# Four head pairs instead of two taken by query halves at the end of a decoder layer, and the order that goes with it

## Chip, core and metric

The kernel runs on one NeuronCore of a Trainium2 chip. The metric is the time of one execution on the device in microseconds (us). TensorE is called PE, VectorE DVE, ScalarE ACT, GpSimd POOL and SyncE SP, as in the profile.

## What is computed

One post-norm decoder layer for 8 batches of 512 rows of width 256: causal linear attention in chunks of 32, cross-attention with 16 heads of 64, and a feed-forward layer with ternary weights and a low-rank gate, each followed by a layer norm of x plus the result.

```python
# linear attention
S = einsum('bncd,bnkd->bnck', Qc, Kc) * mask
out = sigmoid(x @ W_g.T) * O @ W_o.T + x
# cross-attention, 16 heads of 64
a = softmax(einsum('bmhd,bnhd->bhmn', qw, kw) / sqrt(64), axis=-1)
o = einsum('bhmn,bnhd->bmhd', a, vw).reshape(B, M, 1024);  return o @ Wo + bo
# feed-forward: ternary w_fc and w_proj, low-rank gate
h = bitlinear(x, w_fc) + gate * (x @ v.T @ fast_b.T @ u.T)
r = maximum(h, 0);  return bitlinear(r * r, w_proj)
```

## The kernel before

Values of full precision are carried as two fp16 parts (high and low), and products take three passes (high-high, high-low, low-high). Eight batches follow each other. For each batch the steps are:

- `gen_l0`: the linear attention, up to the first norm and the transposed rows `x1T`.
- `gen_kv`, `gen_q`, `gen_v`: keys, queries and values of a head pair (tiles `W`, `v`).
- `scores(u)` for a unit u = (batch, head pair, quarter of the queries; 128 queries): six PE matmuls into two PSUM banks `s`; on DVE per head one custom instruction that adds the mask and takes the minimum (`s`, `nm`), called a score reduction below; on ACT per head one exponential (`e`, with its sum in `den`).
- `split_p`: `e` into the fp16 parts `ph` (high part on ACT or POOL, low part on DVE) and a DMA transpose `pT<-ph` on SP, for two quarters at a time.
- `attend(u)`: 24 small PE matmuls per unit into `av`. With all four quarters in place: division by `den` on DVE (`of`), high part on ACT (`oh`), low part on POOL, a DMA transpose on SP into `oT`.
- `gen_wo`: output projection (`pwo`), second norm, `x2T`; `gen_ffn`: the feed-forward layer (`pz`, `zst`, `ph`, `r`, `rh`, `py`), then the third norm in `ffn_end`.

Work of the neighbouring batches is pulled between the units as filler: projections and the linear attention of batch b+1, output projection and feed-forward of batch b-1.

The last batch (7) ends differently. Its pairs 6 and 7 are "tail" pairs: the units run pair 6 quarters 0 and 1, pair 7 quarters 0 and 1, then the same for quarters 2 and 3. For a tail pair `attend` finishes each half of the queries by itself, with 256-wide instructions and a transpose by PE (`ofl`, `ohl`, `pTo`, copies into `oT` by ACT and DVE). `gen_wo_part` adds the output projection of pairs 0 to 3 early (`pwp`), `wo_tail(i)` that of pairs 4 to 7 for half i (`pwl`) with the second norm (`b`) and its transposes (`pTb`, `x2T`), and `ffn_tail(b, i)` the feed-forward layer of half i, called f0 and f1 below (`pz`, `ph`, `r4` as `r`, `rhl`, `pyl`, `yl`, third norm `c`, output).

The order on each engine is fixed when the program is built. All operations are first recorded (line 454 is the one place that then issues them, so nearly every row of the profile says L454) with a priority: the number of the unit plus offsets. A list scheduler then plays time forward with fixed costs per operation and takes on each engine the ready operation of the lowest priority. `OFF` holds offsets by engine and tile, `TP` those of the tail, `REACH` says how far in priority an engine may look past an operation whose port is taken, `PULL` how much filler is taken per unit. Any change of these numbers can permute the order all over the program.

The end of the recording, before the change:

```python
rest(len(pend) - 4)
wo_tail(0)
f0, f1 = ffn_tail(b, 0, U + TP[1], TP[2]), ffn_tail(b, 1, U + TP[3], TP[4])
go(f0, 3)
...
wo_tail(1)
go(f0, 1)
go(f1, 2)
```

Of the kernel before, what the change touches and what calls it, by code (L numbers as in the profile page):

```python
# [38 lines left out]
OFF = {"ACT th": -0.28, "ACT zst": -1.63, "ACT r": 0.81, "PE pTp": 1.99, "SP pT": 1.41, "ACT sph": 0.41, "DVE zf": 0.49, "PE ph": 0.16, "POOL ph": -1.37, "PE pwp": -0.46, "PE pTb": 2.45, "PE pb": 3.1, "POOL xh": 2.55, "ACT rh": 1.56, "PE pu": 0.39, "ACT row": 1.53, "PE po": -0.14, "PE pwl": 1.81, "SP xs": 0.62, "PE pss": -0.66, "DVE wqkv": -0.5, "DVE fct": -3.44, "ACT oh": -1.55, "DVE sp": 1.14, "POOL rhl": 0.12, "POOL oh": -0.82, "PE pyl": -0.58, "PE pz": -2.5, "PE pp": 0.13, "DVE mvb": -0.45}  # L39
# [436 lines left out]
def decoder_kernel(ctx: ExitStack, tc: tile.TileContext, ins: dict, out: bass.AP):  # L476
# [191 lines left out]
    def setup_ffn():  # L668
# [19 lines left out]
        for i in range(2):  # L688
# [22 lines left out]
        nc.gpsimd.memset(vst, 0.0)  # L711
        split(vst[:, :, 0:RANK], vst[:, :, 96:96 + RANK], sv, WS)
        for g in (32, 64):
            nc.scalar.copy(vst[:, :, g:g + RANK], vst[:, :, 0:RANK])

# [6 lines left out]
        fbs = cst.tile([RANK, 2, 128], F16, name="fbs")  # L722
        nc.gpsimd.memset(fbs, 0.0)
        split(fbs[:, 0, 0:RANK], fbs[:, 1, 0:RANK], fb, 1.0)
        for g in (32, 64, 96):
            nc.scalar.copy(fbs[:, :, g:g + RANK], fbs[:, :, 0:RANK])
        uT = t4("uT", [RANK, 2, HID], F16)
# [7 lines left out]
        for n in range(2):  # L735
# [81 lines left out]
    def to_T(b, row, nm, xT, t0=0, nt=4, fast=False):  # L817
        if fast:
            xf = xT.rearrange("p a c (t n) -> p (a c) t n", t=4)
            for t in range(t0, t0 + nt):  # L820
                xs = wk.tile([128, 2, D], F16, tag="W", name=f"xs{nm}{b}{t}", bufs=4) if b else t4(f"xs{nm}{b}{t}", [128, 2, D])
                nc.scalar.copy(xs[:, 0], row[:, t])
# [167 lines left out]
    def ffn_h(b, j, ts, zst, nm, tail=False):  # L990
# [5 lines left out]
        nc.tensor.matmul(ps, ust[:, js], zst, start=False, stop=True)  # L996
        r4 = wk.tile([128, 256], F32, tag="E", name=f"r4{nm}{j}", bufs=3) if tail else tmp2(f"r4{nm}{j}", [128, ts.stop - ts.start])
        nc.scalar.activation(r4, ps, AF.Relu, scale=sfc4[:, j:j + 1])
# [37 lines left out]
    def ffn_tail(b, i, base, step_):  # L1036
        row = rows[b]
        rh, py = {}, {}
        ts = slice(256 * i, 256 * i + 256)

        rhl = wk.tile([128, 8, 2, 256], F16, tag=("pT", "ph")[i], name=f"rhl{i}", bufs=(PTS, PHS)[i])
        PL = 3
        for s_ in range(8 + PL):
# [3 lines left out]
            if s_ < 8:  # L1047
                j = s_
                r4 = ffn_h(b, j, ts, zst, f"{b}_{i}", True)
                hl = rhl[:, j]  # L1050
                if i == 0 or j % 2:
# [20 lines left out]
        for t in range(2):  # L1072
            tt = 2 * i + t
            y = tmp2(f"yl{tt}", [128, D])
            nc.vector.tensor_tensor(y, py[t], s2b, ALU.mult)
# [13 lines left out]
    def scores(u):  # L1089
# [10 lines left out]
        if qt == 0:  # L1100
            den[b, p] = wk.tile([128, 4, 2], F32, tag="den", name=f"den{b}_{p}", bufs=3)
        e = wk.tile([128, 2, T], F32, tag="E", name=f"e{b}_{p}_{qt}", bufs=3)
# [38 lines left out]
    def attend(u):  # L1141
        b, p, qt = u
        tail = b == B - 1 and p >= NP - 2
        if qt == 0 or (qt == 2 and tail):
# [122 lines left out]
    def step(u):  # L1267
        nonlocal last
        e = scores(u) if u is not None else None
        if last is not None:  # L1270
            nc.prio = now[0] + LATE["s"]
            split_p(*last)
            pend.append(last[0])
        last = (u, e) if u is not None else None

    for i, u in enumerate(units):
# [29 lines left out]
        if qt == 3:  # L1306
# [18 lines left out]
    def wo_tail(i):
        ps = misc(f"pwl{i}")
        for t in (2 * i, 2 * i + 1):
            o = (t - 2 * i) * D
            for p in range(NWP, NP):
                mm(ps[:, o:o + D], lambda k, a: oT[b, p][:, a, t * 128:(t + 1) * 128], lambda k, c: wo[:, p, c, :], 1,  # L1330
                   first=(p == NWP), last=(p == NP - 1))
            nc.vector.scalar_tensor_tensor(row[:, t, :], ps[:, o:o + D], 1.0 / (WS * WS), row[:, t, :], ALU.mult, ALU.add)
            layernorm(b, row, EPS, "b", t, 1, True)
            to_T(b, row, "b", x2T[b], t, 1, True)

    def go(g, n):
        for _ in range(n):
            next(g, None)

    def rest(n):  # L1340
        for _ in range(n):
            if pend:
                attend(pend.pop(0))

    at(U, TP[6])
# [4 lines left out]
    f0, f1 = ffn_tail(b, 0, U + TP[1], TP[2]), ffn_tail(b, 1, U + TP[3], TP[4])  # L1350
    go(f0, 3)
    at(U, 0)
    rest(2)
    go(f0, 3)
    at(U, 0)
    rest(2)
    go(f0, 2)
    at(U, 0)
# [53 lines left out]
```

## Time and profile before

| | |
|---|---|
| time, median of 3 runs | 1062.17 us (1061.53 to 1063.61) |
| the profiled execution's own time | 1060.95 us |
| its span | 1058.8 us (2.15 us lie around it) |
| mean granted PE clock | 0.994 |
| PE matmul busy | 994.6 us (94%), 11976 instructions |
| DVE busy | 985.8 us (93%), 2087 instructions |
| ACT busy | 884.5 us (84%), 1885 instructions |
| POOL busy | 568.7 us (54%), 518 instructions |

How to read it: busy times of one engine are unions of its instructions' spans. A DVE or ACT instruction's span overlaps the next one's by some 0.08 to 0.1 us, so the step from one start to the next is shorter than the duration shown. PE spans are pipelined as well: twelve matmuls of 512 columns by 64 rows show 1.47 us, and one shows 0.38 us. "Idle before" in brackets names the instruction that ended a wait. The span has four parts: set-up up to the first scores (DVE works on them at 49.5 us), eight batches of which the inner ones take some 123.5 us each, and, from 1011.8 us on, when the last score reduction is over, the tail of 47.0 us.

### The profile page before, as it was taken

To read this page: it belongs to the slowest core of one execution; us is meant where nothing else is said; L and a number is where in the kernel's file an instruction comes from. 1 tells how busy PE (TensorE), PEld (TensorE's weight loads), DVE (VectorE), ACT (ScalarE), POOL (GpSimd) and SP (SyncE) were. 2 spreads that over 40 slices of the span, in tenths; PEclk is the share of its full clock that TensorE was granted. 3 is DMA by queue.
4 is the path that set the end of the run, shared out by engine and by line. 5 is a ranking of instruction groups with operands and counts; after the bars stand their busy time and mean duration, and the time that the engine had idled before them with its cause. 6 is when DMAs were issued, how large, how long until landed. Compare 5 with 4: busy or idle time off the path is not lost.

```text
span 1058.8 us, 29904 instructions
## 1 busy us (share of the span) xinstructions
PE 994.6 (94%) x11976; PEld 636.0 (60%) x11976; DVE 985.8 (93%) x2087; ACT 884.5 (84%) x1885; POOL 568.7 (54%) x518
## 2 busy tenths in 40 slices
PE   6987879999999999999999999999999999999996
PEld 4544545665666566765567656665567655565574
DVE  6998999999899989999899999999899998999886
ACT  6797978899986998789987899869987899878846
POOL 0255284256842587344952579425873449424646
PEclk9999999999999999999999999999999999999999
DMA  8359999999999999989999899999999899999971
GB/s 289 119 107 195 186 191 197 178 155 185 194 172 201 164 177 180 203 155 187 173 193 201 158 167 196 187 196 153 180 182 209 147 187 160 187 203 164 174 124 41
DMA packets 646635, 185.64 MB, mean 175 GB/s; under 512 B 628448, under 2 KB 641376, under 8 KB 646496
## 3 DMA queue, kind: packets, MB, share of 16 engines
q1 hardware_dynamic: 644144, 183.34, 94.5%
q8 instruction: 93, 1.52, 0.6%
q10 hardware_dynamic: 2352, 0.40, 0.2%
q14 instruction: 46, 0.38, 0.1%
HBM read 21.18 MB, written 4.19 MB: 24 GB/s over the span
## 4 chain that ended last, share of the span: by engine, by line
PE 48%; DVE 24%; POOL 8%; DMA 8%; ACT 5%; issue 5%; SPq 1%; ACTq 0%; POOLq 0%; DVEq 0%
PE s L454 9%; PE av L454 9%; DVE s L454 8%; DVE ph L454 6%; PE pwo L454 6%; PE pvv L454 5%; PE pk L454 4%; PE pq L454 4%; DMA pT<-ph 4%; PE py L454 3%; DVE W L454 2%; POOL xsa L454 2%; ACT e L454 2%; POOL row L454 2%; PE pxa L454 2%
## 5 line engine op out<-in xcount | busy, mean ns | idle before, releaser
L454 ACT ACTIVATE e<-s,nm 128x512 f32<-128x512 f32 x512 | 350.5, 696 | 79.8 <-DVE nm L454 72.2
L454 DVE SCALAR_TENSOR_TENSOR ph<-e,ph 128x1024 f16<-128x1024 f32 x256 | 334.6, 1310 | 22.7 <-ACT ph L454 20.5
L454 DVE CUSTOM_DVE_ANT_0 s<-s,mb 128x512 f32<-128x512 f32 x512 | 342.1, 706 | 11.0 <-PE s L454 10.0
L454 PEld LDWEIGHTS <-pT 128*128 128x128 f16 x6144 | 197.5, 98 | 60.6 <-issue 37.6
L454 PE MATMUL av<-v,pT 128*128 128x64 f16 x6144 | 212.3, 194 | 12.0 <-DMA pT<-ph 9.7
L454 PE MATMUL s<-W 64*128 64x512 f16 x1536 | 207.4, 379 | 10.7 <-ACT e L454 8.8
L454 ACT ACTIVATE ph<-e 128x1024 f16<-128x1024 f32 x186 | 198.2, 1071 | 2.0
L454 POOL TENSOR_SCALAR ph<-e 128x1024 f16<-128x1024 f32 x70 | 87.5, 1250 | 203.9 <-ACT e L454 187.7
L454 POOL TENSOR_TENSOR oh<-of,oh 128x512 f16<-128x512 f32 x62 | 99.3, 1602 | 92.3 <-ACT oh L454 86.6
L454 PEld LDWEIGHTS <-W 64*128 64x128 f16 x1536 | 64.6, 94 | 108.6 <-issue 53.9
L454 PEld LDWEIGHTS <-wqkv 128*128 128x128 f16 x768 | 68.6, 98 | 88.3 <-issue 27.2
L454 PE MATMUL pk<-ctxh,wqkv 128*128 128x512 f16 x384 | 97.9, 383 | 11.9 <-POOL ctxh L454 8.8
L454 ACT ACTIVATION_READ_ACCUMULATOR e<-s,nm 128x1 f32 x512 | 108.3, 211 | 0.0
L454 PE MATMUL pvv<-wqkv,ctxh 128*128 128x256 f16 x768 | 97.9, 274 | 0.2 <-ACT e L454 0.2
L454 PE MATMUL pq<-x1T,wqkv 128*128 128x512 f16 x384 | 96.1, 380 | 1.3 <-DVE x1T L454 0.7
L454 POOL TENSOR_TENSOR rh<-r,rh 128x512 f16<-128x512 f32 x56 | 76.1, 1367 | 21.2 <-ACT rh L454 20.7
L454 PEld LDWEIGHTS <-oT 128*128 128x128 f16 x768 | 73.4, 98 | 20.9 <-issue 4.8
L454 PEld LDWEIGHTS <-ctxh 128*128 128x128 f16 x768 | 72.8, 98 | 17.4 <-issue 5.9
L454 PE MATMUL pwo<-wo,oT 128*128 128x256 f16 x672 | 82.0, 273 | 0.8 <-ACT e L454 0.5
L454 DVE DVE_READ_ACCUMULATOR2_ANT nm<- 128x1 f32 x512 | 70.0, 137 | 0.0
L454 PE MATMUL ph<-x2T,tfc 128*128 128x512 f16 (+1 forms) x288 | 67.3, 355 | 0.3 <-DVE of L454 0.2
L454 PE MATMUL py<-tpj,rh 128*128 128x256 f16 x448 | 60.3, 273 | 1.3 <-ACT rh L454 1.2
(190 smaller groups left out, 1485.6 us busy)
## 6 DMA issues: line engine op xcount, KB each, us to landing
row<-in_x SPq DMA_DIRECT2D x8, 512.0 KB, 5.8
xs<-in_xT SPq DMA_DIRECT2D x7, 512.0 KB, 4.5
ctxs<-in_ctxT SPq DMA_DIRECT2D x7, 512.0 KB, 4.1
out_dram<-row SPq DMA_DIRECT2D x7, 512.0 KB, 3.5
wqs<-in_wqkv SPq DMA_DIRECT2D x6, 512.0 KB, 8.1
pT<-ph SPq DMA_TRANSPOSE x131, 7.6
wos<-in_wo SPq DMA_DIRECT2D x4, 256.0 KB, 3.2
fcs<-in_w_fc SPq DMA_DIRECT2D x2, 512.0 KB, 4.5
```

Source lines behind the costliest of these rows:

```text
L454: getattr(real[x.engine], x.method)(*[r(a) for a in x.args], **{k: r(a) for k, a in x.kw.items()})
```

## The change

- `NT = 4`: pairs 4 to 7 of batch 7 are tail pairs (before: 6 and 7). The units run quarters 0 and 1 of pairs 4, 5, 6, 7, then quarters 2 and 3 of them. Pairs 4 and 5 take the 256-wide path and PE transposes too.
- `wo_tail(0)` and the generator of f0 are recorded as soon as the first halves of all tail pairs are attended (`start_half`), f0 with a priority from that unit on, and two steps of f0 are taken per unit after that. `wo_tail(1)` and f1 are recorded after f0 is complete; before, f0, `wo_tail(1)` and f1 were recorded interleaved.
- Buffers: f0's `r4` and all `rhl`, `yl`, `ofl`, `ohl`, `xs` tiles use other pools; `den` has 5 buffers instead of 3.
- Set-up: three `memset`, `pjn` (two instructions) from POOL to DVE; the copies `identh`, `s2b`, two `vst`, three `fbs`, two `ust` from ACT to DVE.
- Scheduler numbers: `REACH` 11.86 to 10.35, `PULL["g"]` 4.5 to 4.45, the filler `bw` 3.0 to 8.0 and from pair 7 on, new `TP`, and `OFF` entries for `pTb`, `pu`, `pwl`, `oh` (ACT), `pp` changed and for `x` (SP), `mvc`, `rstdc` added.

```diff
-REACH = 11.86
+REACH = 10.35
...
-TP = (-1.12, 2.0, 1.04, 3.04, 0.1, 5.1, 2.67)
+NT = 4
+FP = 2.0
+TP = (0.0, 1.0, 0.1, 2.0, 0.4, 5.0)
...
-PULL = {"k": 4.41, "l": 2.62, "w": 3.61, "f": 4.71, "g": 4.5}
+PULL = {"k": 4.41, "l": 2.62, "w": 3.61, "f": 4.71, "g": 4.45}
...
-        nc.gpsimd.memset(mdec, 0.0)
+        nc.vector.memset(mdec, 0.0)
...
-        nc.scalar.copy(identh, ident)
+        nc.vector.tensor_copy(identh, ident)
...
-            nc.gpsimd.tensor_scalar(neg, st, th[:, 1:2], None, ALU.is_lt)
+            nc.vector.tensor_scalar(neg, st, th[:, 1:2], None, ALU.is_lt)
...
-        nc.scalar.copy(s2b, pb[:, :D])
+        nc.vector.tensor_copy(s2b, pb[:, :D])
...
-            nc.scalar.copy(ust[64:96, sl], tl[64:96])
+            nc.vector.tensor_copy(ust[64:96, sl], tl[64:96])
...
-        tail = b == B - 1 and p >= NP - 2
+        tail = b == B - 1 and p >= NP - NT
...
+                if p == NP - 1:
+                    pT["done"] = True
...
-    units[-8:] = [(B - 1, p, qt) for q2 in (0, 2) for p in (NP - 2, NP - 1) for qt in (q2, q2 + 1)]
+    units[-4 * NT:] = [(B - 1, p, qt) for q2 in (0, 2) for p in range(NP - NT, NP) for qt in (q2, q2 + 1)]
...
+    def start_half(i):
+        bw.drain()
+        at(i, 1)
+        bf.drain()
+        at(i, TP[0])
+        wo_tail(0)
+        half["f0"] = ffn_tail(B - 1, 0, i + TP[1], TP[2])
...
             for _ in range(BURST - pend[0][2] % BURST):
                 attend(pend.pop(0))
+                if u[0] == B - 1 and "f0" not in half and (B - 1, NP - 1) in av and (B - 1, NP - 1, 1) not in pT and pT.get("done"):
+                    start_half(i)
         at(i, 0.0)
+        if "f0" in half:
+            go(half["f0"], 2)
+            at(i, 0.0)
...
-        if b == B - 1 and p == 6 and qt == 0:
+        if b == B - 1 and p == 7 and qt == 0:
             bw.add(0.0, gen_wo_part, b, NWP)
-        bw.pull(3.0)
+        bw.pull(8.0)
...
+    f0, f1 = half["f0"], ffn_tail(B - 1, 1, U + TP[3], TP[4])
+    at(U, 0)
+    while pend:
+        attend(pend.pop(0))
     at(U, TP[0])
-    rest(len(pend) - 4)
-    wo_tail(0)
...
+    go(f0, 20)
+    at(U, TP[0])
     wo_tail(1)
-    go(f0, 1)
     go(f1, 2)
-    go(f0, 1)
     at(U, TP[5])
-    ffn_end(b - 1)
-    go(f0, 9)
+    ffn_end(B - 2)
     go(f1, 20)
```

More of the change, by code (lines that the diff above doesn't have):

```diff
@@ L35 @@
 NWP = 4
-TP = (-1.12, 2.0, 1.04, 3.04, 0.1, 5.1, 2.67)
+NT = 4
+FP = 2.0
+TP = (0.0, 1.0, 0.1, 2.0, 0.4, 5.0)
 STICK = 2.09
 HOLD = 0.18
-OFF = {"ACT th": -0.28, "ACT zst": -1.63, "ACT r": 0.81, "PE pTp": 1.99, "SP pT": 1.41, "ACT sph": 0.41, "DVE zf": 0.49, "PE ph": 0.16, "POOL ph": -1.37, "PE pwp": -0.46, "PE pTb": 2.45, "PE pb": 3.1, "POOL xh": 2.55, "ACT rh": 1.56, "PE pu": 0.39, "ACT row": 1.53, "PE po": -0.14, "PE pwl": 1.81, "SP xs": 0.62, "PE pss": -0.66, "DVE wqkv": -0.5, "DVE fct": -3.44, "ACT oh": -1.55, "DVE sp": 1.14, "POOL rhl": 0.12, "POOL oh": -0.82, "PE pyl": -0.58, "PE pz": -2.5, "PE pp": 0.13, "DVE mvb": -0.45}
+OFF = {"ACT th": -0.28, "ACT zst": -1.63, "ACT r": 0.81, "PE pTp": 1.99, "SP pT": 1.41, "ACT sph": 0.41, "DVE zf": 0.49, "PE ph": 0.16, "POOL ph": -1.37, "PE pwp": -0.46, "PE pTb": 1.59, "PE pb": 3.1, "POOL xh": 2.55, "ACT rh": 1.56, "PE pu": 1.49, "ACT row": 1.53, "PE po": -0.14, "PE pwl": 2.75, "SP xs": 0.62, "PE pss": -0.66, "DVE wqkv": -0.5, "DVE fct": -3.44, "ACT oh": -3.82, "DVE sp": 1.14, "POOL rhl": 0.12, "POOL oh": -0.82, "PE pyl": -0.58, "PE pz": -2.5, "PE pp": 1.46, "DVE mvb": -0.45, "SP x": 0.75, "DVE mvc": -0.52, "POOL rstdc": -0.86}
 HIGH = ("apaa", "paaa", "papp")
 LATE = {"k": 0.0, "q": 0.0, "v": 0.53, "w": -0.48, "l": -0.41, "o": -0.91, "f": 0.31, "s": 0.0, "a": 0.91, "t": -0.55, "x": 0.31, "e": 0.0, "c": -1.28, "d": -0.95}
-PULL = {"k": 4.41, "l": 2.62, "w": 3.61, "f": 4.71, "g": 4.5}
+PULL = {"k": 4.41, "l": 2.62, "w": 3.61, "f": 4.71, "g": 4.45}
 PASSES = ((0, 0), (0, 1), (1, 0))
@@ L707, in setup_ffn @@
         nc.tensor.matmul(pb[:, :D], ones, dg.rearrange("p a n -> p (a n)"), start=True, stop=True)
-        nc.scalar.copy(s2b, pb[:, :D])
+        nc.vector.tensor_copy(s2b, pb[:, :D])
         yield 6
-        nc.gpsimd.memset(vst, 0.0)
+        nc.vector.memset(vst, 0.0)
         split(vst[:, :, 0:RANK], vst[:, :, 96:96 + RANK], sv, WS)
         for g in (32, 64):
-            nc.scalar.copy(vst[:, :, g:g + RANK], vst[:, :, 0:RANK])
+            nc.vector.tensor_copy(vst[:, :, g:g + RANK], vst[:, :, 0:RANK])
         rs = cst.tile([128, 8], F32, name="rs")
@@ L722, in setup_ffn @@
         fbs = cst.tile([RANK, 2, 128], F16, name="fbs")
-        nc.gpsimd.memset(fbs, 0.0)
+        nc.vector.memset(fbs, 0.0)
         split(fbs[:, 0, 0:RANK], fbs[:, 1, 0:RANK], fb, 1.0)
         for g in (32, 64, 96):
-            nc.scalar.copy(fbs[:, :, g:g + RANK], fbs[:, :, 0:RANK])
+            nc.vector.tensor_copy(fbs[:, :, g:g + RANK], fbs[:, :, 0:RANK])
         uT = t4("uT", [RANK, 2, HID], F16)
@@ L820, in to_T @@
             for t in range(t0, t0 + nt):
-                xs = wk.tile([128, 2, D], F16, tag="W", name=f"xs{nm}{b}{t}", bufs=4) if b else t4(f"xs{nm}{b}{t}", [128, 2, D])
+                xs = wk.tile([128, 2, D], F16, tag="ctxh", name=f"xs{nm}{b}{t}", bufs=2) if b else t4(f"xs{nm}{b}{t}", [128, 2, D])
                 nc.scalar.copy(xs[:, 0], row[:, t])
@@ L996, in ffn_h @@
         nc.tensor.matmul(ps, ust[:, js], zst, start=False, stop=True)
-        r4 = wk.tile([128, 256], F32, tag="E", name=f"r4{nm}{j}", bufs=3) if tail else tmp2(f"r4{nm}{j}", [128, ts.stop - ts.start])
+        r4 = wk.tile([128, 256], F32, tag="E", name=f"r4{nm}{j}", bufs=3) if tail == 2 else tmp2(f"r4{nm}{j}", [128, ts.stop - ts.start])
         nc.scalar.activation(r4, ps, AF.Relu, scale=sfc4[:, j:j + 1])
@@ L1039, in ffn_tail @@
         ts = slice(256 * i, 256 * i + 256)
-        rhl = wk.tile([128, 8, 2, 256], F16, tag=("pT", "ph")[i], name=f"rhl{i}", bufs=(PTS, PHS)[i])
         PL = 3
@@ L1048, in ffn_tail @@
                 j = s_
-                r4 = ffn_h(b, j, ts, zst, f"{b}_{i}", True)
-                hl = rhl[:, j]
+                r4 = ffn_h(b, j, ts, zst, f"{b}_{i}", 1 + i)
+                hl = t4(f"rhl{i}{j}", [128, 2, 256])
                 if i == 0 or j % 2:
@@ L1073, in ffn_tail @@
             tt = 2 * i + t
-            y = tmp2(f"yl{tt}", [128, D])
+            y = wk.tile([128, D], F32, tag="x1T", name=f"yl{tt}", bufs=2)
             nc.vector.tensor_tensor(y, py[t], s2b, ALU.mult)
@@ L1100, in scores @@
         if qt == 0:
-            den[b, p] = wk.tile([128, 4, 2], F32, tag="den", name=f"den{b}_{p}", bufs=3)
+            den[b, p] = wk.tile([128, 4, 2], F32, tag="den", name=f"den{b}_{p}", bufs=5)
         e = wk.tile([128, 2, T], F32, tag="E", name=f"e{b}_{p}_{qt}", bufs=3)
@@ L1157, in attend @@
             if qt % 2:
+                if p == NP - 1:
+                    pT["done"] = True
                 d = den[b, p][:, qt - 1:qt + 1, :]
                 nc.vector.reciprocal(d, d)
-                of = tmp2(f"ofl{p}{qt}", [128, 2, 2, DH])
+                of = wk.tile([128, 2, 2, DH], F32, tag="x1T", name=f"ofl{p}{qt}", bufs=2)
                 nc.vector.scalar_tensor_tensor(of, av[b, p][:, qt - 1:qt + 1], sc, d.unsqueeze(3).broadcast_to([128, 2, 2, DH]), ALU.mult, ALU.mult)
-                oh = tmp2(f"ohl{p}{qt}", [128, 2, 2, 128], F16)
+                oh = wk.tile([128, 2, 2, 128], F16, tag="oh", name=f"ohl{p}{qt}", bufs=1)
                 ofv = of.rearrange("p t h n -> p t (h n)")
@@ L1274, in step, with wo_tail, go @@
         last = (u, e) if u is not None else None
+    half = {}
+    def wo_tail(i):
+        b = B - 1
+        row = rows[b]
+        if i == 0:
+            x2T[b] = wk.tile([128, 2, 2, T], F16, tag="x2T", name=f"x2T{b}", bufs=1)
+        ps = misc(f"pwl{i}")
+        for t in (2 * i, 2 * i + 1):
+            o = (t - 2 * i) * D
+            for p in range(NWP, NP):
+                mm(ps[:, o:o + D], lambda k, a: oT[b, p][:, a, t * 128:(t + 1) * 128], lambda k, c: wo[:, p, c, :], 1,
+                   first=(p == NWP), last=(p == NP - 1))
+            nc.vector.scalar_tensor_tensor(row[:, t, :], ps[:, o:o + D], 1.0 / (WS * WS), row[:, t, :], ALU.mult, ALU.add)
+            layernorm(b, row, EPS, "b", t, 1, True)
+            to_T(b, row, "b", x2T[b], t, 1, True)
+    def go(g, n):
+        for _ in range(n):
+            next(g, None)
+    def start_half(i):
[5 more added lines that the diff above has]
+        half["f0"] = ffn_tail(B - 1, 0, i + TP[1], TP[2])
     for i, u in enumerate(units):
@@ L1302, in decoder_kernel @@
                 attend(pend.pop(0))
+                if u[0] == B - 1 and "f0" not in half and (B - 1, NP - 1) in av and (B - 1, NP - 1, 1) not in pT and pT.get("done"):
+                    start_half(i)
         at(i, 0.0)
+        if "f0" in half:
+            go(half["f0"], 2)
+            at(i, 0.0)
         f = 1 + (0.5 - p % 2) * 0.2
         fr.pull(PULL["k"] + (p % 2 - 0.5) * 3.0)
-        if qt == 3:
+        if qt == 3 or (qt == 1 and i >= len(units) - 4 * NT):
             fr.drain()
@@ L1318, in decoder_kernel @@
     step(None)
-    b = B - 1
-    row = rows[b]
     bw.drain()
-    x2T[b] = wk.tile([128, 2, 2, T], F16, tag="x2T", name=f"x2T{b}", bufs=1)
     U = len(units)
[L1325 to L1345, printed above, removed]
-    bf.drain()
-    at(U, TP[0])
-    rest(len(pend) - 4)
-    wo_tail(0)
[L1350 to L1358, printed above, removed]
+    at(U, 1)
+    bf.drain()
+    if "f0" not in half:
+        start_half(U)
+    f0, f1 = half["f0"], ffn_tail(B - 1, 1, U + TP[3], TP[4])
+    at(U, 0)
+    while pend:
+        attend(pend.pop(0))
+    at(U, TP[0])
+    go(f0, 20)
+    at(U, TP[0])
     wo_tail(1)
-    go(f0, 1)
     go(f1, 2)
-    go(f0, 1)
     at(U, TP[5])
-    ffn_end(b - 1)
-    go(f0, 9)
+    ffn_end(B - 2)
     go(f1, 20)
```

## Prediction

> **What bounds the kernel now.** I read the busy times by stage first, then the waits, then the order of time around the places the change touches. A stage is a window of the span; columns are its length, the busy time (and count) of PE, PE's weight loads, DVE, ACT and POOL, the granted clock, the DMA share and GB/s.
>
> ```profile
> 713.60:837.00 123.40, 120.58 (x1483) 77.29 (x1480) 117.06 (x246) 106.28 (x223) 71.89 (x64) 1.00 0.99 180
> 743.30:767.40 24.10, 21.83 (x254) 13.47 (x253) 20.16 (x35) 23.46 (x49) 21.99 (x19) 1.00 0.91 174
> 957.00:1011.80 54.80, 50.93 (x637) 30.04 (x634) 50.31 (x101) 49.23 (x108) 33.98 (x29) 0.97 1.02 172
> 1011.80:1029.50 17.70, 16.20 (x265) 14.03 (x264) 15.06 (x34) 7.38 (x19) 6.94 (x8) 1.00 0.72 128
> 1029.50:1038.20 8.70, 8.22 (x76) 6.48 (x76) 6.46 (x24) 6.16 (x18) 4.29 (x8) 1.00 0.01 2
> 1038.20:1051.50 13.30, 11.98 (x98) 8.85 (x98) 9.09 (x27) 10.68 (x28) 11.37 (x18) 1.00 0.11 39
> 1051.50:1058.80 7.30, 0.04 (x1) 0.00 (x0) 2.57 (x11) 1.80 (x3) 1.73 (x5) 0.78 0.21 73
> ```
>
> The first row is one inner batch: DVE works 117.1 of 123.4 us, so little is free. The second is the stretch from the scores of pair 6 to those of pair 7: there ACT is busy 23.46 of 24.10 us and sets the pace. The third, from the first score of batch 7, pair 4 to the last score reduction, is the stage that the change reorders: PE 50.9, DVE 50.3 and ACT 49.2 of 54.8 us are all nearly full. The rest is the tail. The order of time gives its milestones and the one regular stall of a batch:
>
> ```profile
> 761.04 1.82 DVE L454 SCALAR_TENSOR_TENSOR ph<-e,ph 128x1024 f16<-128x1024 f32 x1 [3.03 <-ACT ph L454]
> ...
> 1011.68 0.41 DVE L454 SCALAR_TENSOR_TENSOR ofl<-av,den 128x256 f32<-128x256 f32 x1
> ...
> 1029.48 0.60 PE L454 MATMUL pz<-x2T,vst 128*128 128x256 f16 x4
> ...
> 1038.18 0.61 PE L454 MATMUL pz<-x2T,vst 128*128 128x256 f16 x4 [0.48 <-DVE x2T L454]
> ...
> 1050.71 0.83 PE L454 MATMUL pyl<-tpj,rhl 128*128 128x256 f16 x6 [0.37 <-POOL rhl L454]
> ```
>
> Call T the end of the last score reduction, 1011.8. f0 starts (first `pz`) at T+17.7, f1 (second `pz`) 8.7 us later, and from there 20.6 us remain to the end of the span: 47.0 in all.
>
> **What the new order says.** The built program shows the sequence of each engine without times. The name of the change holds in part only: after it, all of f0 still stands behind the last score reduction on DVE, the last exponential on ACT and the last score matmuls on PE. What moves ahead of T is the first half's attention (`ofl`, `ohl`, `pTo` of four pairs), most of `pwl0`, some `py`. Behind it, most of `wo_tail(1)` (the last 12 `pwl`) now stands after the last `pyl` of f0. So f0 starts earlier, f1 no longer overlaps it, and the score stage carries more.
>
> **Set-up.** DVE gains two `pjn`, nine copies and three memsets. The memsets and `identh` lie in DVE's idle time ahead of 8.44 us or just after it: nothing. `pjn` was on POOL:
>
> ```profile
> L454 POOL TENSOR_SCALAR pjn<-pjs,thpj x2: 2842/3270/3698, 89.5 to 102.3; 128x1024 f32<-128x1024 f32 x2
> ...
>   DVE pjt L454: 1.4, 2
> ```
>
> On DVE no row shows it. A 512-wide `mf`/`mb` tensor-scalar steps by 0.34 us, so 0.67 for 1024 if the rate holds; a two-input `ph` row steps by 1.13. I take 0.67, the same kind of instruction: 1.3 us. The other copies, from the nearest rows: five small ones 0.1, two 512-wide `ust` 0.34 (twice the 0.20 step of a 256-wide `rhl` cast), `s2b` 0.33: 1.5. Against that the two waits of `pjt` go (1.4), and the two `ph` beside `pjn` took 2.03 and 1.49 instead of 1.22 (1.1). Net 2.8 - 2.5 = +0.3, between -1 (copies fall into gaps) and +1.9 (`pjn` at 1.13, a third of the relief lost). ACT loses some 2.5 us, but is not what batch 0 waits for.
>
> [...]
>
> **The score stage.** Steps per instruction: 256-wide DVE 0.33, 512-wide 0.60; 64-wide PE 0.029, 128-wide 0.055, 256-wide 0.109. DVE gains 12 instructions of 256 (4.0) and two small reciprocals (0.2) for two `of` of 512 (-1.2): +3.0 of new work. Counting the new order, 1.5 more comes from behind T, and 1.4 from ahead of pair 4's scores: +5.9 in the stage. PE gains 14 to 16 `pTo` (0.9); from behind T come 46 `av` (1.3), 16 `py` (1.7), 6 `pwp` (0.7) and 11 `pwl` (1.2), together 4.8; 1.3 comes from ahead of the stage: +7.0. ACT: +2.4. POOL and SP lose two `oh` (1.2 to 2.0 each) and two `oT` transposes (SP 1.4 each), which nothing waited for here. So PE needs 50.9 + 7.0 = 57.9, DVE 56.2, ACT 51.6. If PE has no gap left, the stage is 57.9; with the 3.9 us of gaps it had, 61.8. The work from ahead of the stage lets it start 1.3 earlier. T moves by 57.9 - 54.8 - 1.3 = +1.8 to 61.8 - 54.8 - 1.3 = +5.7. I take +3.6, between, because three engines that are all near full still wait for each other.
>
> **The tail.** To the first `pz`, DVE has two `y` (1.2), two `ph` (2.3), three 512-wide copies (1.8), 15 of 256 (5.0) and six small (0.5): 10.8. PE's order (34 `py`, 50 `av`, 13 `pwl`, 6.6 us from T-1.4) holds the second `pwl0` row back by 0.9, the norm by 0.4: `pz` at T+12.1 instead of T+17.7. Then ACT is f0's limit: 8 `r` at 0.37, 8 squares at 0.32, 4 `rhl` and an `oT` at 0.30 are 7.0, from 1.4 after `pz`; POOL's last `rhl` 0.65 and `pyl` bring 9.6; 12 `pwl` 1.3: 10.9. From the last `row<-pwl` to `pz` the old tail took 5.9 (1032.30 to 1038.18). The new POOL order puts eight `rstd` instructions and the 4-row one of batch 6 in line ahead of DVE's `x2T`: +1.2. The second `pz` is 18.0 after the first (before 8.7). f1 alone: 1.4, then ACT 8 x 0.37 + 8 x 0.31 = 5.4, 0.4 for three `r4` buffers, 0.8 for the last `rhl` and `pyl`: 8.0; from the last `pyl` to the end 7.4 as before. Total 12.1 + 18.0 + 15.4 = 45.5 against 47.0: -1.5. Bounds: no gain (0), as small waits pile up, or -4 if the `rstd` line and the late `pwl` cost nothing.
>
> **The inner batches.** `REACH` and `OFF` permute DVE, ACT and POOL orders around pairs 5 to 7 of every batch; the work is the same. In the 24.1 us stretch the new DVE order puts four score reductions ahead of four `ph`; walking its rows I get waits of 1.8, 2.1 and 0.9 us on ACT's `ph`, against 3.03 and 0.37. ACT has only 0.6 us free there either way. I take 0, bounds -1.6 to +1 us in each of the five batches that show the stretch.
>
> **Sum.** Against the profiled execution: 1060.95 + 0.3 + 3.6 - 1.5 = 1063.35. That execution is 1.2 below the median 1062.17 of the runs, so the forecast is 1064.6. Within 0.2% (2.1 us) a measurement of this kernel can hardly tell a change.
>
> **Rivals.**
> - Faster: the new order of the inner batches shortens the ACT-paced stretch. For it: `ph<-ACT ph` is the one long DVE stall, DVE is idle 3.9 of its 24.1 us, and ACT idles elsewhere in the batch. Against: ACT's 23.46 us of work stay in it. At 1.6 us in five batches: -8, 1056.6. It decides from 0.9 us each (4.6 us). Chance 0.22.
> - Also faster: f1 keeps its old distance of 8.7 behind f0 while f0 starts 5.6 earlier: 9 us less, 1055.5. Against it stand the 12 `pwl` behind f0 in PE's fixed order. Chance 0.06.
> - Much slower: the score stage keeps all its gaps (+5.7), the tail gains nothing and the set-up costs 1.5: 1069.4. For it: DVE, PE and ACT were all over 89% full and waited in turns. Chance 0.20.
> - Nothing: the 0.2% holds the result because the stage is paced by PE without gaps (T+1.8) and the tail gains its 1.5: 1062.8. Chance 0.12.
>
> The forecast itself has 0.40; its own range 1062 to 1068. Faster by over 0.2% (below 1060.0): both faster rivals but 0.01 short of it, 0.27. Same: the "nothing" case and a part of the forecast (0.08): 0.20. Slower: 0.53. The range, 1056.5 to 1071, leaves out the far ends of three rivals.
>
> **What would show it.** Right: T some 3 us later; first `pz` at T+12, the second 18 us on; DVE busy up by about 5 us in total; `pjt`'s waits gone; 24 us still in the pair 6 to 7 stretch. Wrong: score rows of inner batches at distances other than 123.5 us, the second `pz` within 12 us of the first, or the score stage not longer than before.

## The result and the profile after

The changed kernel takes 1076.9 us (median of 4 runs, 1075.8 to 1079.3) against 1061.85 us before (the 1062.17 above with one more run): ratio 1.0144, 95% interval 1.0129 to 1.016, 15 us slower. A second measurement of it (`changed_again` below) gave 1.0159 (1.0135 to 1.0183). Its profiled execution took 1079.29 us, the longest of the four, with a span of 1077.5 us, 18.7 over the span before. That is some 3.6 more than the medians differ by, mostly because this execution lies 2.4 us above its median and that of the kernel before 0.9 us below its own. Its mean granted PE clock is 0.980, before 0.994.

Windows of the changed kernel, columns as in the prediction: an inner batch, its stretch from pair 6 to pair 7, the score stage, then the tail, cut at the first `pz`, the last `pwl`, the second `pz` and the end of the last `pyl`:

```profile
725.10:848.85 123.75, 121.00 (x1494) 77.76 (x1490) 115.64 (x246) 106.16 (x224) 70.38 (x64) 1.00 1.01 180
754.90:779.20 24.30, 22.16 (x259) 13.93 (x256) 18.40 (x37) 23.28 (x47) 23.82 (x19) 1.00 1.07 194
967.35:1027.00 59.65, 55.34 (x703) 35.64 (x701) 56.96 (x120) 51.11 (x114) 34.49 (x27) 1.00 0.95 170
1027.00:1038.80 11.80, 11.17 (x221) 9.90 (x219) 11.68 (x29) 6.44 (x17) 6.95 (x7) 1.00 0.80 129
1038.80:1050.80 12.00, 11.37 (x96) 8.57 (x95) 5.92 (x17) 7.72 (x23) 4.00 (x6) 1.00 0.00 1
1050.80:1058.30 7.50, 1.25 (x9) 0.60 (x8) 5.87 (x26) 3.75 (x7) 5.43 (x12) 0.79 0.10 35
1058.30:1070.00 11.70, 10.90 (x76) 7.82 (x76) 6.02 (x13) 6.64 (x17) 4.59 (x8) 0.84 0.13 45
```

The score stage is 4.9 us longer, and PE, DVE and ACT are busy there for 4.4, 6.7 and 1.9 us more; as shares of the stage PE is as full as before (93%), DVE fuller (92 to 95.5%) and ACT less full (90 to 86%). New is the sixth row: PE works 1.25 of 7.50 us, and the clock is below 1 there and in the next. The same kernel in order of time, all engines:

```profile
770.36 1.52 DVE L456 SCALAR_TENSOR_TENSOR ph<-e,ph 128x1024 f16<-128x1024 f32 x1 [2.86 <-ACT ph L456]
...
773.73 1.36 DVE L456 SCALAR_TENSOR_TENSOR ph<-e,ph 128x1024 f16<-128x1024 f32 x1 [1.32 <-ACT ph L456]
...
1038.79 0.60 PE L456 MATMUL pz<-x2T,vst 128*128 128x256 f16 x4
...
1055.68 0.40 PE L456 MATMUL pTb<-identh,xsb 128*128 128x128 f16 x2 [4.88 <-ACT xsb L456]
...
1058.31 1.03 PE L456 MATMUL pz<-x2T,vst 128*128 128x256 f16 x4 [0.79 <-DVE x2T L456]
...
1069.14 0.83 PE L456 MATMUL pyl<-tpj,rhl 128*128 128x256 f16 x6 [0.40 <-POOL rhl L456]
```

Four `pz` take 0.60 us the first time and 1.03 the second, where the granted clock is 0.50. To see where the 18.7 us come from, I matched the score reductions of the two traces one by one, by batch and pair:

| part | later by |
|---|---|
| set-up up to the first score reduction | 0.04 |
| batch 0 (first reduction of batch 0 to that of batch 1) | 9.6 |
| batches 1 to 6 together | 2.2 |
| batch 7 up to the end of the last score reduction (T: 1011.8 to 1027.0) | 3.4 |
| tail after T (47.0 to 50.5) | 3.5 |

Half of it sits where the forecast had a third of a microsecond. Within batch 0 the delay appears between pair 4, first quarter (0.33 us late) and pair 5, first quarter (9.08 late). Here is one window of 16 us around that place, first of the kernel before, then of the changed kernel:

```profile
112.00:128.00 16.00, 14.99 (x180) 9.07 (x181) 15.96 (x33) 15.68 (x36) 4.74 (x5) 1.00 0.97 173
```

```profile
112.00:128.00 16.00, 13.96 (x115) 6.67 (x114) 10.78 (x23) 9.83 (x21) 5.41 (x4) 0.68 1.02 176
```

PE is busy 15 and 14 us but does 115 matmuls instead of 180: the granted clock is 0.68. DVE and ACT, at least 98% busy before, wait a third of the time and more. PE's own order, before and after (in brackets: idle time before, and who ended it):

```profile
109.05 1.07 PE L454 MATMUL s<-W 64*128 64x512 f16 x6 [0.29 <-ACT e L454]
110.05 0.39 PE L454 MATMUL pu<-identh,uh 128*16 128x128 f16 x4
110.37 1.13 PE L454 MATMUL s<-W 64*128 64x512 f16 x6
111.71 0.37 PE L454 MATMUL pz<-uT,fbs 16*128 16x512 f16 x1 [0.21 <-ACT uT L454]
112.38 0.38 PE L454 MATMUL pu<-identh,uh 128*16 128x128 f16 x4 [0.30 <-ACT e L454]
...
114.54 1.91 PE L454 MATMUL s<-W 64*128 64x512 f16 x12
```

```profile
108.40 0.60 PE L456 MATMUL pu<-identh,uh 128*16 128x128 f16 x4
...
109.92 0.82 PE L456 MATMUL s<-W 64*128 64x512 f16 x6
110.67 0.39 PE L456 MATMUL pu<-identh,uh 128*16 128x128 f16 x4
111.72 0.37 PE L456 MATMUL s<-W 64*128 64x512 f16 x1 [0.66 <-ACT uT L456]
112.57 0.80 PE L456 MATMUL s<-W 64*128 64x512 f16 x5 [0.47 <-ACT e L456]
...
114.09 0.37 PE L456 MATMUL pz<-uT,fbs 16*128 16x512 f16 x1 [0.40 <-DVE of L456]
115.56 0.83 PE L456 MATMUL pu<-identh,uh 128*16 128x128 f16 x8 [1.10 <-ACT e L456]
...
117.56 1.03 PE L456 MATMUL pz<-uT,fbs 16*128 16x512 f16 x2
118.53 1.46 PE L456 MATMUL s<-W 64*128 64x512 f16 x6
```

Before, 12 matmuls of the third and fourth scores of pair 4 start at 114.54, behind three `pu` blocks. After, all four `pu` blocks and four of the six set-up `pz` stand ahead of the third score; it starts at 118.53. The trace's clock record is at half from 106.3 to 109.7 us (the four `pu` at 108.40 take 0.60 us, those at 110.67 take 0.39) and again from 116.5 to 126.7, where PE's rows take up to 1.8 times as long as at full clock (six `s` 1.46 us at 118.53 against 0.82). No single gap of PE between 100 and 128 us is above 1.51 us.

### The profile page after: what moved, and what is told of

It reads as the page before. It is cut to its first block, busy times and chain, and to the rows that moved or that the text cites. A ratio compares the mean times of both kernels' runs of the same rounds, so it can differ in the third digit from the quotient of the medians.

```text
span 1077.5 us, 30028 instructions
## 1 busy us (share of the span) xinstructions
PE 1005.2 (93%) x11992; PEld 640.6 (59%) x11992; DVE 984.4 (91%) x2113; ACT 881.5 (82%) x1882; POOL 551.7 (51%) x511
## 4 chain that ended last, share of the span: by engine, by line
PE 42%; DVE 18%; ACT 16%; POOL 8%; DMA 8%; issue 6%; SPq 1%; ACTq 0%; POOLq 0%; DVEq 0%
PE s L456 9%; PE av L456 8%; DMA pT<-ph 6%; ACT e L456 5%; ACT r L456 5%; DVE s L456 5%; PE pwo L456 5%; DVE ph L456 5%; PE pvv L456 4%; PE pq L456 3%; PE pk L456 3%; PE py L456 3%; POOL row L456 3%; ACT rh L456 2%; DVE W L456 2%
## 5 line engine op out<-in xcount | busy, mean ns | idle before, releaser
L456 DVE SCALAR_TENSOR_TENSOR ph<-e,ph 128x1024 f16<-128x1024 f32 x256 | 325.3, 1272 | 34.6 <-ACT ph L456 32.4
L456 PEld LDWEIGHTS <-pT 128*128 128x128 f16 x6144 | 201.5, 99 | 62.6 <-issue 35.9
L456 PE MATMUL av<-v,pT 128*128 128x64 f16 x6144 | 216.5, 195 | 9.2 <-DMA pT<-ph 8.2
L456 POOL TENSOR_SCALAR ph<-e 128x1024 f16<-128x1024 f32 x70 | 90.2, 1288 | 206.4 <-ACT e L456 172.7
L456 POOL TENSOR_TENSOR oh<-of,oh 128x512 f16<-128x512 f32 x60 | 83.0, 1383 | 104.4 <-ACT oh L456 104.3
L456 PEld LDWEIGHTS <-W 64*128 64x128 f16 x1536 | 63.6, 94 | 115.2 <-issue 61.8
L456 PE MATMUL pk<-ctxh,wqkv 128*128 128x512 f16 x384 | 100.3, 387 | 7.7 <-ACT e L456 6.6
L456 ACT ACTIVATION_READ_ACCUMULATOR e<-s,nm 128x1 f32 x512 | 106.1, 207 | 0.0
L456 POOL TENSOR_TENSOR rh<-r,rh 128x512 f16<-128x512 f32 x56 | 83.1, 1496 | 34.8 <-ACT rh L456 34.2
L456 PEld LDWEIGHTS <-oT 128*128 128x128 f16 x768 | 73.1, 98 | 21.4 <-issue 4.1
L456 PE MATMUL pwo<-wo,oT 128*128 128x256 f16 x672 | 84.4, 273 | 0.2 <-ACT e L456 0.2
L456 PE MATMUL py<-tpj,rh 128*128 128x256 f16 x448 | 57.2, 273 | 5.1 <-POOL rh L456 4.8
```

The costliest lines, as they stand in the source:

```text
L456: getattr(real[x.engine], x.method)(*[r(a) for a in x.args], **{k: r(a) for k, a in x.kw.items()})
```

## The experiments

Times "over before" are ratio minus 1, times 1061.9 us. Theory A: the set-up's moves cost the 9 us of batch 0. Its rivals: the scheduler's numbers, or only both together.

**Which part of the change costs what.** Four kernels with parts of the diff. `setup_only` is before plus the moved copies, memsets and `pjn`; `numbers_only` is before plus `REACH`, `OFF` and `PULL["g"]`; `tail_only` is before plus all the rest of the diff; `no_setup_moves` is after without the set-up's moves.

```diff
 # setup_only adds these lines to before, no_setup_moves takes them out of after
-            nc.gpsimd.tensor_scalar(neg, st, th[:, 1:2], None, ALU.is_lt)
+            nc.vector.tensor_scalar(neg, st, th[:, 1:2], None, ALU.is_lt)
...
-            nc.scalar.copy(ust[64:96, sl], tl[64:96])
+            nc.vector.tensor_copy(ust[64:96, sl], tl[64:96])
 # numbers_only
-REACH = 11.86
+REACH = 10.35
...
 # tail_only
+NT = 4
+TP = (0.0, 1.0, 0.1, 2.0, 0.4, 5.0)
...
```

> The kernel before with only the set-up's engine moves (pjn, nine copies and three memsets to DVE). Theory A (these moves cost the 9 us that appear between the scores of pair 4 and pair 5 of batch 0, by an order in which all pu and pz of the set-up stand ahead of the third score of pair 4, so that PE falls idle and its granted clock drops): about +9 us, 1071, with the score reductions of pair 5 of batch 0 some 9 us later than before and a granted clock near 0.5 around 116 to 128 us. Rival B (the scheduler's numbers for pu and pp make that order, the moves alone cost what the forecast said): +0.3 us, 1062.4. Rival C (only both together do it): at most +2, 1064.

> The kernel before with only REACH, OFF and PULL g changed. Theory A: +2 us, 1064, all of it in the inner batches, batch 0 as before. Rival B: +11 us, 1073, 9 of them in batch 0. Rival C: +2, 1064.

> The kernel before with only the end changed (four tail pairs, f0 recorded between the second half's scores, other buffers, bw filler, TP); set-up and scheduler numbers as before. If the comparison of the two traces can be carried over: score stage +3.3 and tail +3.5, together +6.8, 1069. If the scheduler's numbers were what made the new end slow (they were chosen with it: pTb, pwl, oh, x, mvc, rstdc): more than +9. If they were chosen to fit something else: less than +4. The forecast's own terms would be +3.6 and -1.5: +2.1, 1064.

> The changed kernel with the set-up's engine moves undone: scheduler numbers and the new end stay. Theory A: the 9 us of batch 0 are gone: +6 us against before (2.2 inner batches, 3.3 score stage, 3.5 tail, less what overlaps), 1068 to 1071. Rival B: as the changed kernel, 1077. Rival C: 1068 to 1071, and setup_only near before.

| | ratio (95%) | over before | pair 5 of batch 0 later by | T later by | first `pz` after T, second after first, rest |
|---|---|---|---|---|---|
| before | | | | | 17.7, 8.7, 20.6 |
| setup_only | 1.0069 (1.0053 to 1.0085) | 7.3 | 3.7 | 6.0 | 19.2, 8.7, 21.4 |
| numbers_only | 1.0039 (1.0023 to 1.0055) | 4.1 | 0.1 | 5.6 | 17.5, 7.5, 21.7 |
| tail_only | 1.0105 (1.0084 to 1.0125) | 11.1 | -0.5 | 3.6 | 18.4, 19.1, 18.7 |
| no_setup_moves | 1.0081 (1.0062 to 1.0099) | 8.6 | 0.9 | 6.1 | 11.8, 19.5, 18.6 |
| changed | 1.0144 (1.0129 to 1.016) | 15.3 | 9.1 | 15.2 | 11.8, 19.5, 19.2 |

Without the set-up's moves the 9 us of batch 0 are gone, and the numbers alone do not make them: so far theory A holds. But its forecast of 9 us for `setup_only` missed: the moves alone make 3.7, and with the numbers 9.1. The rest of the change has no part in that: `tail_only` keeps the order of before on PE, DVE, ACT and POOL up to 960 us. No part gains anything by itself. The numbers belong to the new end: with it they bring the first `pz` from T+18.4 to T+11.8, without it they cost 4.1. So the parts add up to 22.5 and cost 15.3 together.

**The moved instructions or the order made of them.** `moves_old_order` plans all engines' order as if the moved instructions were on POOL and ACT, then issues them on DVE; `new_order_no_moves` does the reverse. PE's order in the first is that of `no_setup_moves`, in the second that of the changed kernel.

```diff
-            nc.vector.tensor_scalar(neg, st, th[:, 1:2], None, ALU.is_lt)
+            nc.pool_as_dve.tensor_scalar(neg, st, th[:, 1:2], None, ALU.is_lt)   # planned on POOL, issued on DVE
...
+                    if x.real:
+                        x.engine = x.real
                     getattr(real[x.engine], x.method)(...)
```

> The changed kernel, but the order of all engines is planned as if the moved set-up instructions were still on POOL and ACT; they are issued on DVE. PE's order is then that of no_setup_moves, instruction for instruction. Theory A1 (the moved instructions cost next to nothing, the forecast's +0.3; what costs is PE's order of pu, pz, pp and scores that the planner makes of the moves): as no_setup_moves, +8.6 over before, 1069 to 1070. Rival A2 (DVE's extra work itself holds the scores back): as the changed kernel, +15, 1076.

> The reverse: the changed kernel with its order as planned, PE's order that of the changed kernel instruction for instruction, but the moved set-up instructions are issued on POOL and ACT as before. A1: as the changed kernel or up to 3 more (pjn waits on POOL are back), +15 to +18, 1076 to 1079. A2: as no_setup_moves, +8.6, 1069.5.

Measured: 1.0113 (1.0091 to 1.0135) and 1.0153 (1.0128 to 1.0178). The same window of `moves_old_order`, then of `new_order_no_moves`:

```profile
112.00:128.00 16.00, 14.49 (x175) 7.97 (x174) 15.95 (x35) 15.93 (x36) 4.29 (x5) 1.00 1.01 175
```

```profile
112.00:128.00 16.00, 13.57 (x103) 6.17 (x100) 11.22 (x23) 11.03 (x26) 5.45 (x4) 0.67 0.97 165
```

With the instructions on DVE and PE's old order the clock stays at 1.00 and pair 5 is 0.55 us late, no more than in `no_setup_moves` (0.89). With the instructions back on their old engines and PE's new order it is 9.84 us late, and the time is 7.6 us above `no_setup_moves`. The 9 us are the order's, not the instructions'. The instructions are not free, though: `moves_old_order` missed its +8.6 and is 3.4 us above `no_setup_moves` (their intervals overlap), of which its trace has 3.1 between pair 5 of batch 0 and batch 1, with the clock at 0.64 in 140 to 144 us. The mean granted clock of its four runs is 0.983 to 0.987, in `no_setup_moves` 0.988 to 0.991. How the instructions bring this about was not shown.

**The clock or the waits.** The changed kernel with 2.2 us of extra PE work where PE idles, in two ways; all other orders stay. `fill_batch0` repeats narrow matmuls (`pu`, 16 columns of weights; `pz`, 16 rows); `fill_full` issues ten matmuls of 128 rows, 128 columns and 512 wide.

```diff
 # shortened; fill_batch0: the second pu block 4 times, the first pz matmul 3 (n=0) and 6 (n=1) times
-                    getattr(real[x.engine], x.method)(...)
+                    for i in range(again(x)):
+                        getattr(real[x.engine], x.method)(...)
...
 # fill_full: ahead of the second pu block 3, of the first pz matmuls 2 and 5
+                    for _ in range(FILL(x)):
+                        nc.tensor.matmul(pu, identh, wqkv[:, 0, 0, 0, 0:512], start=True, stop=True)
                     getattr(real[x.engine], x.method)(...)
```

> The changed kernel with the second pu block issued 4 times, the first pz matmul of n=0 3 times and of n=1 6 times (each overwrites with the same values): about 2.2 us more PE work just where PE was idle 2.1 us between 110 and 116 us; every other order unchanged. Theory K (the idle PE lowers its granted clock, and the half clock from 116 to 128 us costs 3 to 5 of the 9 us): 3 to 5 us less than the changed kernel, +10 to +12 over before, clock 0.9 or more in those windows. Rival (order and bank waits alone, or the clock follows something earlier): +15 to +17, clock again near 0.5.

> The changed kernel with ten matmuls of full size (128 rows, 128 columns of weights, 512 wide, some 0.22 us each; 3 before the second pu block, 2 and 5 before the first pz matmuls; overwritten by what follows) where PE idles between 110 and 116 us; all orders else unchanged. Fill_batch0 put narrow matmuls there (16 columns or 16 rows of the array), PE was busy and the clock fell nevertheless. Theory K2 (what holds the clock is work of the array, and pu and pz, which use an eighth of it, count as idle): clock 0.9 or more from 112 to 128 us, pair 5 of batch 0 some 4 to 5 us later than before instead of 9, +10 to +12 over before. Rival (the clock follows what lies ahead of 110 us, or the delay is bank waits and order alone): +15 to +17, clock again near 0.5.

`fill_batch0` missed: 1.0153 (1.0133 to 1.0173), no gain. `fill_full` gave 1.0126 (1.0111 to 1.0142). The window of `fill_batch0`, then of `fill_full`:

```profile
112.00:128.00 16.00, 16.00 (x153) 8.34 (x152) 10.48 (x22) 10.24 (x23) 5.66 (x4) 0.68 0.99 164
```

```profile
112.00:128.00 16.00, 16.00 (x181) 8.22 (x180) 15.41 (x32) 14.39 (x30) 6.64 (x5) 1.00 1.01 173
```

PE is busy all 16 us in both, and the clock is 0.68 in one and 1.00 in the other. In order of time, the eight `pu` that both have next:

```profile
113.41 1.02 PE L459 MATMUL pu<-identh,uh 128*16 128x128 f16 x8
```

```profile
114.35 0.61 PE L459 MATMUL pu<-identh,uh 128*16 128x128 f16 x8
```

The busy share ahead of the fall does not tell the two apart either. In `fill_batch0` the clock fell at 112.9 us; here is the stretch before that in `fill_batch0`, then in `fill_full`:

```profile
108.00:112.00 4.00, 3.04 (x28) 1.65 (x27) 4.00 (x9) 3.10 (x7) 0.00 (x0) 1.00 1.14 218
```

```profile
108.00:112.00 4.00, 3.03 (x24) 1.03 (x20) 4.00 (x11) 3.02 (x8) 0.00 (x0) 1.00 1.06 201
```

In the profiled execution of `fill_full` pair 5 is 3.00 us late instead of 9.08, its own filler included. In that of `fill_batch0` it is 6.43 us late, with the clock at half for 10.24 us instead of the 13.65 of the changed kernel; its median shows none of that gain. The gain of `fill_full` in the medians was small, and the changed kernel had not run beside it, so I repeated it, with a stronger filler and on the other order (`fill_more`: 20 fillers; `fill_setup_only`: 12 fillers in `setup_only`, two more than its expectation says):

> The changed kernel itself, beside the next runs on the same chip: 1.4 to 1.6% over before.

> fill_full again, beside the changed kernel. Theory K2 (half the delay of batch 0 is PE's half clock, kept away by full-size matmuls in its gaps, in most executions): 3 to 6 us less than the changed kernel. Rival (the 6 us of the one profile were chance): within 1 us of it.

> As fill_full with twenty instead of ten fillers (2.2 us more PE work), also before the first, third and fourth pu blocks. K2: clock at 1 in 100 to 128 us in this profile too; the time about that of fill_full, since the added work costs what the clock still gives. Rival: 2 us slower than fill_full.

> setup_only (+7.1 over before; its clock fell to 0.50 at 116 to 120 us) with ten full-size fillers: 3 before the second pu block, 5 before the third, 2 before each first pz matmul. K2: clock 0.9 or more from 108 to 128 us, pair 5 of batch 0 at most 2 us later than before (there 3.7), +4 to +5.5 over before. Rival: as setup_only or 2 more, +7 to +9.

Side by side: changed 1077.63 us, 1.0159 (1.0135 to 1.0183); `fill_full_again` 1073.19 us, 1.0111 (1.0091 to 1.013). So 4.4 us go although 2.2 us of work are added, and it holds beyond the profiled execution: the mean granted clock of its five runs is 0.988 or 0.989, of the four of `changed_again` 0.978 to 0.983. Its profile has the clock at 1.00 from 96 to 144 us and pair 5 late by 3.19, where `changed_again` has 0.57 in the window and 9.94. `fill_setup_only`: 1.0043 (1.0025 to 1.006) against 1.0069 (intervals overlap), clock 1.00 from 96 to 144 us, pair 5 late by 1.13 instead of 3.72. `fill_more` missed: 1.0144 (1.0121 to 1.0168). Its clock had already fallen to 0.72 in 104 to 108 us, ahead of all its filler (the first at 107.8 us), and it does 2.2 us more. The same early fall, of 3.41 us from 105.5 to 107.2 us on, stands in the profiles of the changed kernel, `changed_again` and `new_order_no_moves`, where it is longer still (6.83 us), and not in those of `fill_full`, `fill_full_again` and `fill_batch0`, whose filler also comes only behind it. So the filler cannot be what kept that one away; why it comes in some and not in others was not shown. 3.41 us at half clock are worth at most 1.7 us of PE's work (estimate from that length).

**The tail: the clock.** Matmuls into a bank that nobody reads, put into PE's order of `no_setup_moves` behind the last `pwl` (`tail_fill`: 40 of 256 columns; `tail_fill2`: 46, and 8 more behind the last `pTb`).

```diff
+            if t == 3:
+                fill(40)    # tail_fill2: fill(46) here, fill(8) behind to_T
             nc.vector.scalar_tensor_tensor(row[:, t, :], ps[:, o:o + D], ...)
```

> no_setup_moves with 40 matmuls of 256 columns (4.4 us, into a bank that nobody reads) put into PE's order behind the last pwl, where PE waits 4.9 us for the norm of the second half; all else in the same order. Theory K: PE's clock stays at 1, pTb, pz and the ph of f1 run at full rate, second pz 0.5 to 1 us earlier, pz to end 16 to 17 instead of 18.6: 2 to 3 us less than no_setup_moves, +6 over before. Rival (f1 is a chain of ACT, DVE and POOL, PE's clock is beside it): as no_setup_moves, +8.6, within 0.5.

> no_setup_moves with 46 filler matmuls behind the last pwl and 8 more behind the last pTb, in front of the second pz (tail_fill had 40 and none, and its clock fell to 0.70 at 1048 to 1052, just behind the filler). Theory K: pz and the first ph of f1 at full clock (4 pz 0.6 instead of 1.0 us, 11 ph 1.4 instead of 2.6), 1.5 to 2.5 us less than no_setup_moves, +6 to +7. Rival (the chain over ACT, DVE and POOL sets f1): +8 to +9, within 0.5 of no_setup_moves.

`tail_fill` missed its 2 to 3 us: 1.0069 (1.0043 to 1.0094), its tail 50.0 us after T as in `no_setup_moves` (50.0); the clock was 1.00 beside the filler and fell to 0.70 behind it, at 1048 to 1052 us. `tail_fill2`: 1.0053 (1.0036 to 1.007), clock 1.00 up to 1060 us, tail 48.3 us. The first `r` of f1 in `no_setup_moves` (second `pz` at 1049.18) and in `tail_fill2` (second `pz` at 1050.43), order of time on ACT:

```profile
1052.74 1.20 ACT L456 ACTIVATE r<-ph,sfc 128x256 f32<-128x256 f32 x3 [2.11 <-PE ph L456]
```

```profile
1052.39 1.21 ACT L456 ACTIVATE r<-ph,sfc 128x256 f32<-128x256 f32 x3 [0.94 <-PE ph L456]
```

From `pz` to `r` it is 3.56 us at half clock and 1.96 at full clock. That 1.6 us is what the clock costs in the tail of this execution; the ratios, not measured side by side, agree in direction only.

**The tail: the order.** The last attention units and `wo_tail(1)` of `no_setup_moves` get priorities ahead of f0's body; in `before_new_end_early` the same is done to `tail_only`.

```diff
-    at(U, 0)
+    at(half["i"], 0.5)          # the unit at which f0 was started
     while pend:
         attend(pend.pop(0))
-    at(U, TP[0])
-    go(f0, 20)
-    at(U, TP[0])
+    at(half["i"], -2.5)
     wo_tail(1)
+    at(U, TP[0])
+    go(f0, 20)
```

> no_setup_moves with the last attention units and wo_tail(1) given priorities ahead of f0's body, so that the second half's norm runs beside f0 and the second pz stands among the last pyl of f0, as in the kernel before. Theory D (the end lost its overlap of f1 with f0 by order, not by need): second pz 9 to 12 us after the first instead of 19.5, tail 44 to 47 us behind the last score reduction instead of 50, 3 to 6 us less than no_setup_moves: +3 to +6 over before. Rival (ACT, DVE and POOL are shared, f0 gets later by as much): at most 1 less than no_setup_moves, +7.5 to +9.

> Set-up and scheduler numbers of before, the new end, and the second half early as in second_half_early: what is left of the change when the parts shown to cost are taken out. Theory D: score stage +3, tail 44 to 47 instead of 56 of tail_only: 0 to +4 over before. Rival: as tail_only, +9 to +11. Faster than before by over 0.2% would need a tail below 42 us.

`second_half_early`: 1.0062 (1.0042 to 1.0082). PE's two `pz` in it:

```profile
1032.47 0.60 PE L456 MATMUL pz<-x2T,vst 128*128 128x256 f16 x4
...
1042.80 0.49 PE L456 MATMUL pz<-x2T,vst 128*128 128x256 f16 x3 [0.78 <-DVE x2T L456]
```

The second `pz` comes 10.3 us after the first instead of 19.5, the tail is 46.9 us after T instead of 50.0. But from the second `pz` to the end it then takes 23.4 us instead of 18.6, and T came 1.5 later in this execution, so the time falls by 2 us only, and within the intervals. `before_new_end_early`: 1.0048 (1.0029 to 1.0066) against 1.0105 of `tail_only`: T only 0.7 later than before, `pz` at T+18.4, 11.7, 21.2. Its expected 0 to +4 and tail of 44 to 47 us missed: +5.1 and 51.2. It has the lowest ratio of the kernels with the new end (that of `tail_fill2`, 1.0053, lies within its interval), and is still 5 us slower than before.

## Why the prediction was right or wrong

The direction was right, and the size was missed by 12 us; 1076.9 lies beyond the range. The direction is in part luck: the forecast put the loss into the score stage, which has 3.4 of the 15 us, and most of it came from elsewhere. Step by step, in the profiled executions:

- **Set-up, +0.3: the step that failed.** The prices hold where a row shows them. `pjn` on DVE steps by 0.66 us (forecast 0.67), `s2b` by 0.33 (0.33), the waits of `pjt` are gone:

```profile
90.57 0.75 DVE L456 TENSOR_SCALAR pjn<-pjs,thpj 128x1024 f32<-128x1024 f32 x1
...
108.48 0.41 DVE L456 COPY s2b<-ps 128x256 f32<-128x256 f32 x1
```

  In PE's old order the moved instructions cost nothing up to pair 5 (`moves_old_order` 0.55 us late, `no_setup_moves` 0.89). But the step priced instructions in a fixed order, and the planner made a new one. The forecast read the new order for the score stage, the tail and pairs 5 to 7, and not for batch 0, where all four `pu` blocks and four `pz` now stand ahead of the third score, before three and one. In that order batch 0 takes 9.6 us longer, and the order alone (`new_order_no_moves`) 9.5; the upper bound of +1.9 took no account of it. Even in the old order the moves come to 3.4 us in the medians, lost behind pair 5, where the clock had fallen (0.64 in 140 to 144 us).
- **What the forecast lacked altogether is PE's clock.** It treated a matmul's duration as fixed and PE's gaps as worth their own length. Of the 9 us some 4 to 6 are the half clock (9.08 to 3.00 in the profiles, of which an estimated 1.7 us at most belong to the early fall, which the filler does not touch; in the medians 4.4, after 2.2 us of added work). In the tail the clock fell at 1055.2 us, 4.4 us into a PE gap of 4.88 us, and the four `pz` behind it took 1.03 us against 0.60. In batch 0 it fell with no gap above 1.51 us, and in `fill_batch0` in a window with PE busy 16.00 of 16 us. No long gap was needed there: short gaps and narrow matmuls stood ahead of the fall, and with ten wide matmuls in the gaps (`fill_full`) the clock stayed at 1.00 in that window.
- **Score stage, T +3.6: right in size, in part by luck.** 3.4 was measured in batch 7, the stage took 59.65 us (forecast between 57.9 and 61.8). PE's work was put 2.6 too high (57.9, measured 55.3), DVE's (56.2, 57.0) and ACT's (51.6, 51.1) fit; the stage kept 4.3 us of PE gaps, as it had 3.9, where the middle of the forecast left about 2. The two errors cancel.
- **Tail, -1.5: wrong, +3.5.** First `pz` at T+12.1: 11.8, right. Second `pz` 18.0 later: 19.5. From there 15.4: 19.2. Most mis-sized is f1 alone, 8.0 forecast, 11.7 measured: its first `r` came 3.6 us after `pz` instead of 1.4, and 1.6 of that is the half clock (`tail_fill2`). That f1 no longer overlaps f0 was foreseen, and order, not need, did it (`second_half_early`); of the 9.2 us by which the second `pz` comes nearer to the first, 4.8 are lost from there to the end and 1.4 in a later first `pz`.
- **Inner batches, 0: nearly right.** The stretch of pair 6 takes 24.3 to 24.6 us in batches 3 to 6 before and 24.4 us after; the three waits on ACT's `ph` are 2.86, 1.32 and 0.68 us, 4.9 in sum, forecast 4.8. Batches 1 to 6 together lost 2.2.
- **The rivals.** The two faster ones did not happen: ACT's stretch kept its length, and f1 lost its distance to f0. "Much slower" had the right sign, from the score stage's gaps, which was the wrong place.

Open: why the moves cost 3.4 us in the old order too. Why the numbers deepen the delay from 3.7 to 9.1 us was seen only as a longer time at half clock (6.83 us in `setup_only`, 13.65 in the changed kernel). After batch 0's pairs there is a second place, 140 to 164 us, where the clock falls in all profiles that were read there, for a length that varies from kernel to kernel (mean granted clock from 128 to 172 us 0.96 in the kernel before and 0.88 in the changed one); what it costs was not measured by itself.

## What to carry to other kernels

Where a planner fixes the order, moving a cheap instruction means a new order for all engines near it: read that order on the engine that sets the pace, there first, or plan with the old engines and issue on the new ones. Before filling or thinning a stretch of TensorE, look at its granted clock as well as its busy share: in the changed kernel short gaps (none above 1.51 us) between narrow matmuls were followed by a clock of 0.50 for the wide ones behind them (six `s` in 1.46 us instead of 0.82). Numbers that were fitted to one end of a kernel do not carry to another; parts of such a change have to be measured together and apart.

## What the hardware showed that I had not expected

- In the changed kernel and `setup_only` the granted PE clock fell to 0.50 between 100 and 128 us with no PE gap above 1.8 us there, and PE's busy share did not tell when it falls. From 100 to 106 us PE was busy 4.46 us in the changed kernel, whose clock fell at 106.3, and 3.79 us in the kernel before, whose clock stayed at 1.00. From 108 to 112 us it was busy 3.04 us in `fill_batch0`, whose clock fell at 112.9, 3.03 us in `fill_full` and 3.12 us in the kernel before, where it stayed at 1.00. `fill_full`, with 2.2 us of wide matmuls in the gaps, kept 1.00 from 112 to 128 us in both of its profiles; `fill_batch0`, with 2.2 us of narrow ones (16 columns or 16 rows), fell to 0.68 over that window. In that window PE was busy all 16.00 us in both, so the clock did not hold behind the narrow matmuls here and held with the wide ones; no counter shows why.
- The clock has two values in these traces, 1.00 and 0.50, and the half clock comes in stretches of 3.41 us (the kernel before), 6.83 and 10.24 (the changed kernel) or 13.65 (`changed_again`), multiples of 3.41; only the last of a profile, which runs past the program's end, has another length. Shares such as 0.68 are means over a window.
- In `tail_fill` the filler held the clock only while it ran: behind 4.5 us of it the clock was down again 3.1 us later, with light PE work between (filler to 1046.5 us, half clock from 1049.6).
- A fallen clock did not always cost: `tail_only` lost more clock in batch 0 than before (0.52 at 88 to 92, 0.50 at 152 to 156 us) and was only 0.7 us later at batch 1.
